# Expert products of layer 0: which scheduling turns may carry them

## The chip, the cores and the metric

The kernel runs on one core of a Trainium2 chip, as one launch. The metric is the device time of that launch in microseconds, from start to end, inputs and outputs in device memory. Three runs of the kernel before gave 3691.05, 3695.77 and 3702.05 us; their median, 3695.77 us, is the time to compare with.

## What is computed

The input is 16 samples of 512 tokens with 128 features in float32. Two layers follow each other. Cut to what matters:

```
xn = layernorm(x)
x  = x + memory(xn) + block0(xn)      # layer 0
xn = layernorm(x)
x  = x + attention1(xn) + moe1(xn)    # layer 1
```

- `memory` is a small two-layer network whose weights are updated over 8 chunks of 64 tokens, one after the other (a scan), and then read out.
- `block0` is a convolution over tokens, attention with 16 heads of width 8, a layernorm, and a dense mixture of 8 experts with 512 hidden units each: every token goes through every expert.
- `attention1` is causal attention with 16 heads, a convolution, and a second causal attention with the same keys and values.
- `moe1` sends each token to 8 of 32 small experts.

The dense mixture of layer 0 is what the change touches:

```
h = relu(einsum('bsd,edf->bsef', x, w1) + b1)
y = einsum('bsef,efd->bsed', h, w2) + b2
moe_out = einsum('bse,bsed->bsd', probs, y)
```

## The kernel before

The whole network is written as stages (Python generators), and a class `Turns` runs them. In every turn each live stage does one small step and gives control back. TensorE executes its instructions exactly in the order in which the turns issue them; so the list of turns, fixed when the program is built, is TensorE's program. There are 1279 turns. The launch falls into three parts: up to turn 520 the attention of layer 0 beside the scan; from turn 520 the attention of layer 1, with layer 0's expert products still going on; from turn 1140 the end of layer 1 and its own experts.

Within a turn the stages come in the order of a priority:

1. `tops` (priority 0) calls `largest`: two score matmuls of 64 rows (four or eight narrower ones near the causal corner), whose row maxima VectorE takes. In the profile these matmuls are `s<-kx,qx`. The maxima make the softmax safe.
2. `back` (priority 1) calls `weighted`: the same scores a second time, transposed, in the profile `s<-qx,kx`. ScalarE turns them into exponentials (line 470, tile `e`). The score tile has one buffer only (tag `p2`, `pools["p2"]` is 1), so the scores of the next turn cannot be written before ScalarE has read this turn's. In layer 1 GpSimd then cuts the causal corner (line 474).
3. Still in `weighted`, or in `summed` (priority 2) at the end of a head group, `tail` sums attention values: matmuls `pc<-e,vp`, one for each head, four or eight heads at once, when enough exponentials have gathered. A turn in which this happens puts the word `"values"` into `locks`. I call it a values turn, and any other turn a plain turn.
4. Other stages (priorities 3 to 5): the scan, projections, convolutions, layernorms, transposes.
5. `experts0` (priority 6) calls `ffn` for one sample after the other: the expert products.

One sample's expert products are 64 pieces: `first(i)` is a product of 128 hidden units for all 512 tokens (`phe<-x1T,ew`), followed by a relu on ScalarE (line 584) into `hTe`; `second(i)` multiplies that back to 128 features (`pye<-ew,hTe`, line 594), and every fourth one scales the sum by the gate on ScalarE (line 601) and adds it up on GpSimd (line 602). For 16 samples that is 1024 pieces. The two stand alternately: a `first`, then the `second` of the `first` before.

How many pieces a turn gets is decided in `ffn` by a credit. Each turn adds 2750 ns (`TURN`) to the credit and takes off `load_ns`, an estimate of the TensorE time of everything else in the turn; each piece takes off 1000, and the credit is capped at 4000, so at most four pieces are due at once. The kernel before then has two more rules. With `pools["pairs"]`, which is true throughout, the number of pieces is rounded down to an even one in plain turns, and set to zero in values turns unless four are due. And where the maxima of a turn keep VectorE longer than TensorE (`look_ns` against `load_ns`), pieces are added to fill the difference.

A last helper, `fill` (line 203), issues an otherwise useless matmul in turns with little TensorE work, but only when no expert stage has run for more than two turns.

Of the kernel before, what the change touches and what calls it, by code (L numbers as in the profile page):

```python
# [73 lines left out]
def bc(ap, axis, n):  # L74

    u = ap.unsqueeze(axis)
    shape = list(u.shape)
    shape[axis] = n
    return u.to_broadcast(shape)
# [3 lines left out]
def network(ctx: ExitStack, tc: tile.TileContext, a, out):  # L83
# [26 lines left out]
    def load(pool, name, shape):  # L110
        t = pool.tile(shape, F32, bufs=1, name="sb_" + name)
        nc.sync.dma_start(t, a[name])
        return t
# [22 lines left out]
    def col(name, i=0):  # L136
        k = COLS[name] + i
        return cols[:, k : k + 1]

    pools, done, locks, clock, newest, cleared, held, read, cell = {}, {}, set(), [0], [None], [None], [0], [0], []  # L140
# [3 lines left out]
    def mark(*m):  # L144
        done[m] = clock[0]

    def after(*marks, lag=0):

        while not all(m in done and clock[0] >= done[m] + lag for m in marks):
            yield  # L150
# [12 lines left out]
    def room():  # L163

        while held[0] >= pools["work"]:
            yield

    def hold(name):

        held[0] += 1  # L170
        return work(name)

    def drop():

        read[0] += 1

    def work(name):
        return pools["ps"].tile([P, 512], F32, tag="bank", bufs=5, name=name)

    def toks(ap):  # L180
        return ap.rearrange("p (t d) -> p t d", d=P)

    def flat(ap):
        return ap.rearrange("p t d -> p (t d)")

    load_ns, look_ns, array_ns, at_ffn = [0.0], [0.0], [0.0], [-9]

    def mm(o, lhsT, rhs, start=True, stop=True):
        n = int(np.prod(rhs.shape[1:]))
        if lhsT.dtype == FR:  # L190
            load_ns[0] += 0.5 * (0.45 * n + 105)
        else:
            t = 0.42 * n if lhsT.shape[-1] == 32 and n >= P else 2 * max(0.834 * n, 110)
            load_ns[0] += t
            array_ns[0] += t
        nc.tensor.matmul(o, lhsT=lhsT, rhs=rhs, start=start, stop=stop)  # L196
# [72 lines left out]
    def idle(n):  # L269
        for _ in range(n):  # L270
            yield
# [240 lines left out]
    credit, fetched = [0.0], {}  # L512
# [9 lines left out]
    def fetch0(b):  # L522

        x1T = ff.tile([P, S], F32, tag="x1T", bufs=1, name="x1T")
        nc.sync.dma_start(x1T, x1d[1, b])
        fetched[b] = x1T, {}, {}
        fetch1(*fetched[b][1:], 0)
        fetch2(*fetched[b][1:], 0)

    def ffn(b):  # L530

        yield from after(("x1", b))
        ac = ff.tile([P, TB, D], F32, tag="x1", bufs=1, name="ac")
        nc.sync.dma_start(flat(ac), x1d[0, b])
        if b not in fetched:
            fetch0(b)
            yield from idle(3)
        x1T, w1, w2 = fetched.pop(b)
        padded = gates0[b % 2]
        pr = padded[:, 0 : TB * EXP0].rearrange("p (t e) -> p t e", e=EXP0)  # L540
        prT = ff.tile([P, P], F32, tag="y", bufs=2, name="prT")

        def gate():
            yield from room()
            pgt = hold("pgt")[:, 0 : TB * EXP0].rearrange("p (t e) -> p t e", e=EXP0)
            for t in range(TB):
                mm(pgt[:, t, :], x1T[:, t * P : (t + 1) * P], gw0)
            yield
            mx = sm.tile([P, TB], F32, tag="mx", name="mx")
            nc.vector.tensor_tensor(pr, pgt, bc(row["gb"][:, 0:EXP0], 1, TB), ALU.add)  # L550
            drop()
            nc.vector.tensor_reduce(mx, pr, AX.X, ALU.max)
            nc.vector.tensor_tensor(pr, pr, bc(mx, 2, EXP0), ALU.subtract)
            yield
            nc.scalar.activation(pr, pr, AF.Exp)
            yield
            sp = sm.tile([P, TB], F32, tag="sp", name="sp")
            nc.vector.tensor_reduce(sp, pr, AX.X, ALU.add)
            nc.vector.reciprocal(sp, sp)
            nc.vector.tensor_tensor(pr, pr, bc(sp, 2, EXP0), ALU.mult)  # L560
            yield
            yield from room()
            ptp = work("ptp")
            nc.tensor.transpose(ptp[:, 0:P], padded, ident)
            nc.scalar.copy(prT, ptp[:, 0:P])
            yield from idle(2)
            yield from room()
            pb2 = work("pb2")
            mm(pb2, prT, eb2)
            y = ff.tile([P, TB, D], F32, tag="y", bufs=2, name="y")  # L570
            nc.scalar.copy(flat(y), pb2)
            nc.gpsimd.tensor_tensor(ac, ac, y, ALU.add)
            yield

        hs, pye, n = {}, [None], 4 * EXP0

        def first(i):
            e, f = divmod(i, 4)
            if e + 1 < EXP0 and f < 2:
                (fetch1, fetch2)[f](w1, w2, e + 1)  # L580
            ph = work("phe")
            mm(ph, w1[e][:, f * P : (f + 1) * P], x1T)
            hs[i] = ff.tile([P, S], F32, tag="hTe", bufs=3, name="hTe")
            nc.scalar.activation(hs[i], ph, AF.Relu, bias=col("fb", i))  # L584
            if i == n - 1 and ("x1", b + 1) in done:
                fetch0(b + 1)

        def second(i):
            e, f = divmod(i, 4)
            h = hs.pop(i)  # L590
            if f == 0:
                pye[0] = toks(hold("pye"))
            for t in range(TB):
                nc.tensor.matmul(  # L594
                    pye[0][:, t, :], lhsT=h[:, t * P : (t + 1) * P], rhs=w2[e][:, f, :],
                    start=(f == 0 and t == 0), stop=(f == 3), skip_group_check=True,
                )
            if f == 3:
                y = ff.tile([P, TB, D], F32, tag="y", bufs=2, name="y")
                for t in range(TB):  # L600
                    nc.scalar.mul(y[:, t, :], pye[0][:, t, :], pr[:, t, e : e + 1])  # L601
                nc.gpsimd.tensor_tensor(ac, ac, y, ALU.add)  # L602
                drop()

        units = [(first, 0)]
        for i in range(1, n):
            units += [(first, i), (second, i - 1)]
        units.append((second, n - 1))
        gating, at = gate(), 0
        while at < len(units):  # L610

            at_ffn[0] = clock[0]
            credit[0] = min(credit[0] + TURN - load_ns[0], 4000)
            more = int(max(credit[0] + 500, 0) // 1000)
            if pools["pairs"]:
                more = more // 2 * 2 if "values" not in locks or more > 3 else 0
            if credit[0] > -2000:

                more = max(more, int((look_ns[0] - load_ns[0] - 400) / 1000 + 0.7))
            for fn, u in units[at : at + more]:  # L620

                if held[0] >= pools["work"] - (fn is second and u % 4 == 0):
                    break
                fn(u)
                at += 1
                credit[0] -= 1000
            next(gating, None)
            yield
        yield
        nc.sync.dma_start(x1d[0, b], flat(ac))  # L630
        mark("ffn", b)
        yield
# [6 lines left out]
    att = main.enter_context(tc.tile_pool(name="att", bufs=1))  # L639
    fa = main.enter_context(tc.tile_pool(name="fa", bufs=2))  # L640
    ff = main.enter_context(tc.tile_pool(name="ff", bufs=1))
    ps = main.enter_context(tc.tile_pool(name="psum", bufs=1, space=PSUM))
    pools.update(ps=ps, p2=1, work=3, weights=[att], heads=4, pairs=True)
    Wt = Pack(load(fa, "pb", [P, sum(PB.values())]), PB)
    cell.append(Wt.t)
    row.update(load_rows(fa, "rows0", ROWS0))
# [485 lines left out]
    def experts0():  # L1132
        for b in range(B):
            yield from ffn(b)
# [26 lines left out]
        pass  # L1161
    for _ in padded_values(l1, 2):
        pass
    pools["pairs"] = True

    def middle(mid, b):

# [435 lines left out]
```

## Time and profile before

| What | Value |
|---|---|
| median of three runs | 3695.77 us |
| profiled execution, its own time | 3697.03 us |
| span in its profile | 3695.3 us |
| granted TensorE clock, mean | 0.970 |
| TensorE busy | 3466.2 us (94%) |
| VectorE / ScalarE / GpSimd busy | 62% / 58% / 43% |
| instructions | 62879 |

The span runs from the first to the last instruction; the profiled execution took 1.7 us more than its span. Busy shares are means over the three parts. "PE" is TensorE's matmuls, "PEld" its weight loads, "DVE" VectorE, "ACT" ScalarE, "POOL" GpSimd, "SP" the queue that issues most DMAs.

### The profile page before, as it was taken

To read this page: it belongs to the slowest core of one execution; us is meant where nothing else is said; L and a number is where in the kernel's file an instruction comes from. 1 tells how busy PE (TensorE), PEld (TensorE's weight loads), DVE (VectorE), ACT (ScalarE), POOL (GpSimd) and SP (SyncE) were. 2 spreads that over 40 slices of the span, in tenths; PEclk is the share of its full clock that TensorE was granted. 3 is DMA by queue.
4 is the path that set the end of the run, shared out by engine and by line. 5 is a ranking of instruction groups with operands and counts; after the bars stand their busy time and mean duration, and the time that the engine had idled before them with its cause. 6 is when DMAs were issued, how large, how long until landed. Compare 5 with 4: busy or idle time off the path is not lost. (4 is left out here: it accounts for less than half of the span.)

```text
span 3695.3 us, 62879 instructions
## 1 busy us (share of the span) xinstructions
PE 3466.2 (94%) x22209; PEld 1925.9 (52%) x22209; DVE 2283.0 (62%) x5907; ACT 2154.0 (58%) x3703; POOL 1571.3 (43%) x2524
## 2 busy tenths in 40 slices
PE   6999999899999899999999999999999999998877
PEld 3445554454555455455555555555555665443443
DVE  5676656556756565566466666666666666777652
ACT  1556756665656687666566666666666665443433
POOL 5433532442431455432444344434443444443664
PEclk7999999899999999999999999999999999998998
DMA  5222222222223233443434443444344334333343
GB/s 171 68 69 74 80 77 65 68 74 82 65 66 94 85 114 93 122 120 105 135 96 132 121 125 110 120 124 127 101 124 130 114 107 116 96 99 95 84 85 85
DMA packets 290074, 370.83 MB, mean 100 GB/s; under 512 B 46016, under 2 KB 141408, under 8 KB 289376
## 3 DMA queue, kind: packets, MB, share of 16 engines
q1 hardware_dynamic: 282592, 359.99, 34.0%
q0 software_dynamic: 7168, 6.82, 1.1%
q8 instruction: 177, 2.90, 0.3%
q14 instruction: 137, 1.12, 0.1%
HBM read 236.85 MB, written 133.25 MB: 100 GB/s over the span
## 5 line engine op out<-in xcount | busy, mean ns | idle before, releaser
L470 ACT ACTIVATE e<-s 128x1024 f32<-128x1024 f32 (+1 forms) x1216 | 1190.9, 979 | 667.7 <-PE s L196 587.0
L399 DVE TENSOR_REDUCE nm<-s 128x1 f32<-128x512 f32 (+2 forms) x1408 | 906.9, 683 | 527.0 <-PE s L196 525.6
L391 DVE CUSTOM_DVE_ANT_0 s<-s,sb_const 128x512 f32<-128x512 f32 (+1 forms) x1024 | 624.3, 643 | 444.3 <-PE s L196 436.3
L474 POOL TENSOR_SCALAR_AFFINE_SELECT e<-e 128x128 f32<-128x128 f32 (+2 forms) x1408 | 467.0, 367 | 865.9 <-ACT e L470 859.5
L196 PE MATMUL s<-kx,qx 64*128 64x512 f32 (+3 forms) x3072 | 657.3, 430 | 58.8 <-DVE nm L399 14.6
L196 PE MATMUL pc<-e,vp 128*32 128x512 f32 (+3 forms) x6144 | 657.2, 506 | 43.9 <-POOL e L474 41.8
L196 PEld LDWEIGHTS s<-kx,qx 64*128 64x128 f32 x3072 | 293.1, 187 | 627.9 <-issue 251.9
L594 PEld LDWEIGHTS pye<-ew,hTe 128*128 128x128 f32 x4096 | 517.7, 192 | 174.0 <-issue 159.5
L196 PE MATMUL s<-qx,kx 64*128 64x512 f32 (+3 forms) x3072 | 533.2, 360 | 39.4 <-ACT e L470 27.6
L594 PE MATMUL pye<-ew,hTe 128*128 128x128 f32 x4096 | 564.6, 281 | 0.8 <-ACT hTe L584 0.8
L196 PE MATMUL phe<-x1T,ew 128*128 128x512 f32 x1024 | 539.9, 612 | 8.4 <-DVE nm L399 6.4
L584 ACT ACTIVATE hTe<-phe,sb_cols 128x512 f32<-128x512 f32 x512 | 352.8, 690 | 280.5 <-PE phe L196 278.3
L602 POOL TENSOR_TENSOR ac<-ac,y 128x512 f32<-128x512 f32 x128 | 164.5, 1285 | 408.8 <-ACT y L601 380.9
L196 PEld LDWEIGHTS s<-qx,kx 64*128 64x128 f32 x3072 | 294.6, 189 | 82.0 <-ACT e L470 57.0
L398 DVE TENSOR_TENSOR s<-s,sb_const 128x256 f32<-128x256 f32 (+1 forms) x384 | 180.9, 516 | 230.6 <-PE s L196 224.9
L196 PEld LDWEIGHTS pc<-e,vp 128*32 128x32 f32 x6144 | 155.5, 110 | 285.5 <-issue 173.1
L196 PEld LDWEIGHTS phe<-x1T,ew 128*128 128x128 f32 x1024 | 157.7, 192 | 59.8 <-issue 34.2
L601 ACT ACTIVATE y<-pye,pr 128x128 f32<-128x128 f32 x512 | 146.8, 368 | 30.8 <-PE pye L594 25.8
L203 PE MATMUL fill<-sb_pb,sb_const 128*128 128x512 f32 (+2 forms) x324 | 148.4, 547 | 10.9 <-DMA sb_pb<-in_pb 10.3
L391 DVE DVE_READ_ACCUMULATOR2_ANT nm<- 128x1 f32 x1024 | 144.6, 141 | 0.0
L209 POOL TENSOR_SCALAR rs_t<-ss 128x4 f32<-128x4 f32 (+1 forms) x56 | 11.9, 213 | 238.8 <-ACT sq L262 235.1
L209 POOL TENSOR_SCALAR rs_t<-ln_mv 128x4 f32<-128x4 f32 x64 | 12.7, 198 | 178.7 <-DVE ln_mv L219 176.4
(292 smaller groups left out, 3856.0 us busy)
## 6 DMA issues: line engine op xcount, KB each, us to landing
ew<-in_ew SPq DMA_DIRECT2D x256, 256.0 KB
kx<-rk SPq DMA_DIRECT2D x192, 256.0 KB
qx<-rq SPq DMA_DIRECT2D x128, 256.0 KB
rq<-hi SPq DMA_DIRECT2D x64, 256.0 KB
rq<-lo SPq DMA_DIRECT2D x64, 256.0 KB
rk<-hi SPq DMA_DIRECT2D x64, 256.0 KB
rk<-lo SPq DMA_DIRECT2D x64, 256.0 KB
qx<-r SPq DMA_DIRECT2D x64, 256.0 KB
```

The source lines that it names most:

```text
L196: nc.tensor.matmul(o, lhsT=lhsT, rhs=rhs, start=start, stop=stop)
L203: nc.tensor.matmul(o[:, 0:n], lhsT=ident, rhs=cell[0][:, 0:n], start=True, stop=True)
L209: nc.gpsimd.tensor_scalar(t, src, scale, eps, ALU.mult, ALU.add)
L391: newest[0] = nc.vector.tensor_tensor_reduce(out=sv[r][:, 0, :], in0=sv[r][:, 0, :], in1=row["caus"][:, S - n :], scale=1.0, scalar=-BIG, ...
L398: nc.vector.tensor_tensor(dg, dg, bc(row["caus"][:, S - P :], 1, per), ALU.add)
L399: newest[0] = nc.vector.tensor_reduce(nm[:, qt, r, t : t + per], sv[r], AX.X, ALU.max)
L470: nc.scalar.activation(e[:, :, 0 : per * n], s[:, :, 0 : per * n], AF.Exp, scale=SCALE)
L474: cleared[0] = nc.gpsimd.affine_select(out=ev[:, r, :, 0:P], in_=ev[:, r, :, 0:P], pattern=[[0, per], [1, P]], compare_op=ALU.is_ge, fill= ...
L584: nc.scalar.activation(hs[i], ph, AF.Relu, bias=col("fb", i))
L594: nc.tensor.matmul(pye[0][:, t, :], lhsT=h[:, t * P : (t + 1) * P], rhs=w2[e][:, f, :], start=(f == 0 and t == 0), stop=(f == 3), skip_gro ...
L601: nc.scalar.mul(y[:, t, :], pye[0][:, t, :], pr[:, t, e : e + 1])
L602: nc.gpsimd.tensor_tensor(ac, ac, y, ALU.add)
```

## The change

Both extra rules go away and one takes their place. In a values turn, as many pieces as the credit says are due are issued, up to four and without rounding; since `ffn` has the lowest priority, they stand behind the value matmuls of that turn. In a plain turn pieces are issued only when four are due, and then four. The addition by `look_ns` is gone.

```diff
             credit[0] = min(credit[0] + TURN - load_ns[0], 4000)
             more = int(max(credit[0] + 500, 0) // 1000)
-            if pools["pairs"]:
-                more = more // 2 * 2 if "values" not in locks or more > 3 else 0
-            if credit[0] > -2000:
-
-                more = max(more, int((look_ns[0] - load_ns[0] - 400) / 1000 + 0.7))
+            if "values" not in locks and more < 4:
+                more = 0
             for fn, u in units[at : at + more]:
...
-    pools.update(ps=ps, p2=1, work=3, weights=[att], heads=4, pairs=True)
+    pools.update(ps=ps, p2=1, work=3, weights=[att], heads=4)
...
-    pools["pairs"] = True
```

## The prediction, made before the changed kernel ran

> **What bounds the kernel now.** I read the page's busy rows first, then the busy times of each part, then TensorE's timeline turn by turn. The page says that TensorE is nearly always busy, from shortly after the start to about 3100 us, and much less afterwards:
>
> ```profile
> PE 3466.2 (94%) x22209; PEld 1925.9 (52%) x22209; DVE 2283.0 (62%) x5907; ACT 2154.0 (58%) x3703; POOL 1571.3 (43%) x2524
> ...
> PE   6999999899999899999999999999999999998877
> ...
> PEclk7999999899999999999999999999999999998998
> ```
>
> The same by part. The first row runs from turn 520 to the last pieces, the second is the stretch right after them:
>
> ```profile
> 1604.00:3104.00 1500.00, 1474.51 (x10555) 876.57 (x10554) 923.81 (x2837) 926.12 (x1483) 616.26 (x1293) 1.00 0.42 119
> 3104.00:3290.00 186.00, 170.92 (x1187) 83.33 (x1185) 137.42 (x426) 91.52 (x117) 80.48 (x197) 0.94 0.38 102
> ```
>
> TensorE is busy 98% with pieces, 92% without, and there most plain turns carry a `fill`. So the pieces do not just add work: they stand where TensorE would otherwise wait. TensorE's timeline shows what for. Columns: start, duration, then instruction and count; a bracket is idle time and what ended it.
>
> ```profile
> 1774.79 0.51 PE L196 MATMUL s<-qx,kx 64*128 64x512 f32 x2
> 1775.23 0.66 PE L248 MATMUL tpc<-sb_const,cs 128*128 128x128 f32 x4
> 1776.49 0.51 PE L196 MATMUL s<-qx,kx 64*128 64x512 f32 x2 [0.61 <-ACT e L470]
> 1776.93 1.16 PE L594 MATMUL pye<-ew,hTe 128*128 128x128 f32 x8
> 1777.92 1.02 PE L196 MATMUL phe<-x1T,ew 128*128 128x512 f32 x2
> 1778.78 1.05 PE L594 MATMUL pye<-ew,hTe 128*128 128x128 f32 x8
> 1779.67 1.02 PE L196 MATMUL phe<-x1T,ew 128*128 128x512 f32 x2
> 1780.63 0.45 PE L196 MATMUL s<-qx,kx 64*128 64x384 f32 x2
> ```
>
> The second score pair waits 0.61 us because the exponential of the first still reads the only score buffer: 1.70 us from one pair to the next, however little TensorE has to do. After it four pieces fit before the next scores, from 1776.93 to 1780.63, with nothing waiting. Call the distance from scores to scores the exp cycle. Its parts are the pair (0.40), the exponential (1.02 for 1024 columns, 0.81 for the 384-wide turns) and two handovers (about 0.15 together). That is 1.6 us in layer 0 and about 1.5 in layer 1, where 4 of 11 turns are 384 wide; I use 1.55.
>
> ```profile
> 2202.95 0.49 PE L196 MATMUL s<-kx,qx 64*128 64x512 f32 x2
> 2203.28 0.34 PE L196 MATMUL s<-qx,kx 64*128 64x384 f32 x2
> 2203.55 1.16 PE L594 MATMUL pye<-ew,hTe 128*128 128x128 f32 x8
> 2204.54 1.02 PE L196 MATMUL phe<-x1T,ew 128*128 128x512 f32 x2
> 2205.49 0.50 PE L196 MATMUL s<-kx,qx 64*128 64x512 f32 x2
> ```
>
> This is the commonest plain turn before: both score pairs and a pair of pieces, 2205.49 - 2202.95 = 2.54 us (2.55 is the median of such turns). The exponential runs under the pieces and costs nothing. The same turn with four pieces lasts 4.31 us (2085.3 to 2089.6, for one), so a further piece costs (4.31 - 2.55)/2 = 0.88 us. The bare scores take 0.60 (2202.95 to 2203.55), which leaves 2.55 - 0.60 - 1.76 = 0.19 us for going into a group of pieces and out of it.
>
> **The change part by part.** The turns are the same 1279 in the same order; only pieces move. The instruction order of the two programs, cut into turns, gives:
>
> - pieces in values turns: 57 before, 741 after; in plain turns 967 before, 283 after (sum 1024 both)
> - values turns that carry pieces: 46 and 277; plain turns that do: 426 and 75
> - last piece: turn 1057 and turn 1080, still ahead of turn 1140, where the last sample's next stage starts; that delay costs nothing
> - plain turns with no piece: 237 more than before, up to turn 1080. Of them, 186 have nothing but scores on TensorE (59 before turn 520, 127 after), 91 have a little more (mostly the 256- and 128-wide score turns), 70 have at least 1.5 us of other work (some emptied turns are offset by others filled, so these are net counts by kind).
>
> *A bare turn emptied of a pair.* It falls from 2.55 to the exp cycle, 1.55: minus 1.00. Its two pieces go behind values, where TensorE has no slack (a values turn with eight heads spends 1.92 us on `pc` beside the scores), and cost 2 x 0.88 = 1.76. Net +0.76 us, the group overhead of 0.19 saved in it. The gap is counted once per emptied turn, so a turn that lost four counts the same. 186 x 0.76 = 141 us.
>
> *A turn with a little more.* The 256-wide pair turns lasted 2.98, so their own work is about 1.0; emptied they fall to 1.55: -1.43 + 1.76 = +0.33. The 128-wide ones lasted 2.82. In the stretch without pieces eight of them took a median of 2.06 (VectorE ends those): -0.76 + 1.76 = +1.0, at least +0.5 if 1.55 holds. The rest of this kind gain or lose nothing. With roughly 27, 33 and 31 turns of the three sorts: 9 + 33 + 0, about 41 us.
>
> *The 70 others.* Their own TensorE work exceeds the cycle; a pair cost 1.7 there, as behind values. Zero.
>
> *What else moves with the pieces.* Relu and gate scaling go with them on ScalarE: 0.69 for each `first`, four times 0.29 for each expert sum. They lie ahead of the next exponential in ScalarE's queue. Before, pieces hid that; now a relu that trails its values turn ends before the next scores do (0.9 us of scores), but a trailing gate scaling delays the exponential by about 0.3, in at most 128 places: 0 to 38 us, I take 15. GpSimd's cut of the causal corner gets less cover before the values that need it. The stretch without pieces shows it, `pc` waiting 0.85 us:
>
> ```profile
> 3106.55 0.99 PE L196 MATMUL pc<-e,vp 128*32 128x256 f32 x8 [0.85 <-POOL e L474]
> ```
>
> It cost 2.7 us in 30 values turns there; over 190 in layer 1, 17 us, between 0 and 60. The 256 expert weight loads move on SP with their pieces. Each is asked for at least seven pieces ahead, now about two values turns or 17 us; no wait on them shows in the trace, and I cost them at nothing. If that cover went, each landing would be paid on TensorE. Twelve `fill`s fewer: nothing.
>
> **A rule against the row: the clock.** The trace shows the clock halved after a thin window, although the gap in it was short:
>
> ```profile
> 3173.90:3177.30 3.40, 1.14 (x18) 0.38 (x10) 1.65 (x6) 0.94 (x1) 1.22 (x2) 1.00 0.56 119
> 3177.30:3180.70 3.40, 3.34 (x6) 1.34 (x8) 0.00 (x0) 1.02 (x1) 0.54 (x2) 0.50 1.08 239
> 3180.70:3184.10 3.40, 3.40 (x26) 1.90 (x28) 1.95 (x4) 1.61 (x2) 0.54 (x2) 0.50 0.30 51
> ```
>
> TensorE had been busy 1.14 of 3.40 us, with one gap of 2.32. The Trainium skill ("TensorE: Matmul & The Clock Gate", section "HAM oscillation — how this bites in real kernels") asks only that no idle gap pass about 3.4 us. By the rule the new gaps, about 1 us each, cost nothing. By the row a thin window is enough. A lone emptied turn between two values turns leaves the window about two thirds full; two in a row, 23 times in layer 1, may leave it thin. Half of these at 3.4 us of half clock: 12 x 1.7 = 20 us. If all 226 gaps counted half the time it would be 190. I go with the row and take 10.
>
> A second page speaks for the change ("TensorEngine Tiling (Array Packing)", "Key Properties"): changing the tiling mode drains TensorE. Scores (64*128), values (128*32) and pieces (128*128) are three modes; by my count about 450 changes fewer. The row prices a group's entry and exit at 0.19 us, and that is already in the +0.76. By the rule alone, with TensorE never waiting, the sum would be a gain (third rival).
>
> Sum: 141 + 41 + 15 + 17 + 10 = 224, less about 25 for emptied turns whose gap falls into a wait that exists already (PE waits for 15 us on ACT e and 11 on DVE nm in the first part): +200 us. From the profiled execution's 3697 that is 3897; the median lies 1 us lower, so 3896.
>
> **The rivals.**
>
> 1. *The exp cycle is only half exposed* (9%): other work follows the scores more often than I counted, and the first part hides its 59 gaps behind the scan. Then about +90, 3786. For it: the first part has waits of up to 10 us. Against: layer 1 has almost none, and holds two thirds of the sum.
> 2. *The clock joins in* (15%): thin windows halve it after most emptied turns, +60 to +190 on top: 3950 to 4080. For it: the rows above. Against: scores keep TensorE more than half busy in the cycle.
> 3. *Fewer mode changes win* (4%, faster): 351 plain groups dissolve at 0.19 us, 231 groups join values at perhaps half of that: -67 + 22 = -45, 3651. It decides if TensorE can use the emptied time, which needs an exp cycle under about 0.8 us instead of 1.55. The wait of 0.61 above says no.
> 4. *No change to measure* (2%): the cycle's cost and the saved mode changes cancel.
>
> **How the numbers follow.** The main case has 70%, with its own range from 3800 to 3990. Taking in the first rival and the lower part of the second, 3790 to 4010 leaves out about 2 in 10. About 0.3% is what a measurement here can tell from no change. Slower 0.94, within it 0.02, faster 0.04.
>
> **What would show it.** TensorE busy falls from 98% to about 90% in the part from turn 520 on, with new entries "PE s <- ACT e" of some 100 us in the waits, where 10.7 stood; plain bare turns at 1.5 to 1.7 us, values turns at 4 to 6. ScalarE and VectorE keep their busy times. It is wrong if that wait stays small, if the clock in that part falls well under 1.00, or if the loss lies before turn 520.

## The result: 3963 us, 7.1% slower

| Kernel | Median | Lowest to highest | Runs |
|---|---|---|---|
| before | 3698.91 us | 3691.05 to 3703.94 | 4 |
| changed | 3962.86 us | 3961.11 to 3969.10 | 4 |

The ratio is 1.0711 (95% interval 1.0699 to 1.0724): 264 us lost where +200 was forecast, inside the range of 3790 to 4010.

The three parts, cut at the first score matmul of turns 90, 520 and 1058 in each trace:

| Part | Before | Changed | Difference |
|---|---|---|---|
| turns 90 to 520 | 1347.0 us | 1395.0 us | +48.0 |
| turns 520 to 1058 | 1499.7 us | 1692.6 us | +192.9 |
| turn 1058 to the end | 591.0 us | 614.6 us | +23.6 |

Pieces moved between the parts too. The first part has 308 pieces before and 307 after, the second 716 and 685, the end none and 32. So the middle loses its 193 us with 31 pieces less to do (about 27 us at 0.88 each), and the +23.6 at the end comes with 32 more (about 28).

### The profile page after: what moved, and what is told of

It is laid out like the page before. It is cut to its first block, busy times and chain, and to the rows that moved or that the text cites. A ratio compares the mean times of both kernels' runs of the same rounds, so it can differ in the third digit from the quotient of the medians.

```text
span 3959.7 us, 62838 instructions
## 1 busy us (share of the span) xinstructions
PE 3550.3 (90%) x22185; PEld 1973.2 (50%) x22185; DVE 2265.3 (57%) x5907; ACT 2160.7 (55%) x3703; POOL 1578.9 (40%) x2524
## 5 line engine op out<-in xcount | busy, mean ns | idle before, releaser
L196 PE MATMUL s<-kx,qx 64*128 64x512 f32 (+3 forms) x3072 | 684.7, 423 | 93.2 <-issue 32.7
L196 PE MATMUL pc<-e,vp 128*32 128x512 f32 (+3 forms) x6144 | 685.5, 526 | 40.6 <-POOL e L474 40.4
L196 PE MATMUL s<-qx,kx 64*128 64x512 f32 (+3 forms) x3072 | 559.6, 376 | 179.2 <-ACT e L470 165.6
L594 PEld LDWEIGHTS pye<-ew,hTe 128*128 128x128 f32 x4096 | 529.2, 194 | 235.2 <-issue 208.9
L196 PEld LDWEIGHTS s<-kx,qx 64*128 64x128 f32 x3072 | 318.4, 188 | 563.6 <-issue 272.3
L203 PE MATMUL fill<-sb_pb,sb_const 128*128 128x512 f32 (+2 forms) x300 | 140.1, 558 | 10.9 <-DMA zrow<-zero 10.4
```

What stands on the lines that cost most here:

```text
L203: nc.tensor.matmul(o[:, 0:n], lhsT=ident, rhs=cell[0][:, 0:n], start=True, stop=True)
L594: nc.tensor.matmul(pye[0][:, t, :], lhsT=h[:, t * P : (t + 1) * P], rhs=w2[e][:, f, :], start=(f == 0 and t == 0), stop=(f == 3), skip_gro ...
```

## The profile after

The page's busy rows, with the 40 slices of TensorE. TensorE has slightly more busy time than before and a lower share, and the steady level 9 of the middle is gone:

```profile
PE 3550.3 (90%) x22185; PEld 1973.2 (50%) x22185; DVE 2265.3 (57%) x5907; ACT 2160.7 (55%) x3703; POOL 1578.9 (40%) x2524
...
PE   6999999989999999988989889889898889998887
```

The same stretch as before, from turn 520 to 1058, is now:

```profile
1652.00:3345.00 1693.00, 1511.47 (x10392) 887.52 (x10391) 902.97 (x2834) 915.43 (x1452) 617.03 (x1292) 0.97 0.37 105
```

TensorE was idle for 1500.0 - 1474.5 = 25.5 us there before and is idle for 1693.0 - 1511.5 = 181.5 now. So 156 of the 193 us are waiting. Busy time rose by 37 although 31 pieces left, so the work that stayed takes some 64 us longer; the clock column, 0.97 instead of 1.00, belongs here. VectorE, ScalarE and GpSimd do nearly what they did.

What TensorE waited for in that stretch (total us, times, longest):

```profile
PE s L196 <- ACT e L470: 105.6, 158, 1.4
PE s L196 <- issue: 31.1, 20, 1.6
PE s L196 <- DVE nm L399: 12.4, 21, 1.6
PE s L196 <- DVE nm L391: 6.0, 12, 0.6
...
PE pc L196 <- POOL e L474: 2.1, 2, 1.2
```

Before, the first of these lines was:

```profile
PE s L196 <- ACT e L470: 10.7, 13, 1.2
```

The exponential holds scores up for 105.6 us instead of 10.7. A second group, 31.1 + 12.4 + 6.0 = 49.5 us, is first scores that wait for a bank which VectorE's maxima have not yet given back. The view puts the 31.1 us under "issue", to no engine; but each of these 20 waits, 1.51 to 1.58 us long, ends 0.10 us after a maximum of VectorE (line 399) has ended. So of the 156 us of new waiting about 95 end with the exponential and nearly 50 with VectorE.

From one values turn to the next on TensorE's timeline (the bracket is idle time and its end):

```profile
2092.11 0.44 PE L196 MATMUL s<-kx,qx 64*128 64x384 f32 x2
2092.39 0.40 PE L196 MATMUL s<-qx,kx 64*128 64x256 f32 x4
2092.63 0.33 PE L196 MATMUL s<-kx,qx 64*128 64x384 f32 x2
2093.99 0.66 PE L196 MATMUL s<-qx,kx 64*128 64x128 f32 x8 [1.03 <-ACT e L470]
2094.58 1.07 PE L196 MATMUL pc<-e,vp 128*32 128x256 f32 x16
2095.59 1.12 PE L196 MATMUL phe<-x1T,ew 128*128 128x512 f32 x2
2096.55 1.05 PE L594 MATMUL pye<-ew,hTe 128*128 128x128 f32 x8
2097.44 1.02 PE L196 MATMUL phe<-x1T,ew 128*128 128x512 f32 x2
```

A plain turn issues its two score groups (2092.11 and 2092.39), the next turn's maxima scores follow at once (2092.63), and then nothing can be done for 1.03 us: from 2092.39 to 2093.99, one exp cycle of 1.60 us. Then come values and three pieces, all without a gap. At the same place in the kernel before, four pieces stood between the two score groups, and the values turn behind them carried none:

```profile
1999.07 0.40 PE L196 MATMUL s<-qx,kx 64*128 64x256 f32 x4
1999.40 1.12 PE L196 MATMUL phe<-x1T,ew 128*128 128x512 f32 x2
2000.36 1.05 PE L594 MATMUL pye<-ew,hTe 128*128 128x128 f32 x8
2001.25 1.02 PE L196 MATMUL phe<-x1T,ew 128*128 128x512 f32 x2
2002.11 1.05 PE L594 MATMUL pye<-ew,hTe 128*128 128x128 f32 x8
...
2003.37 0.56 PE L196 MATMUL s<-qx,kx 64*128 64x128 f32 x8
```

Without them the turn shrank from 4.30 to 1.60 us, which is 2.70 less; four pieces at 0.88 elsewhere cost 3.52.

## The experiments

**The rule in one part only.** The kernel before with the new rule from turn 520 on.

```diff
+            if clock[0] >= 520:
+                if "values" not in locks and more < 4:
+                    more = 0
+            else:
                 ...
```

> The new rule from turn 520 on, the old one before it. If the loss is made turn by turn, by emptied plain turns, the parts add: turns 90 to 520 last 1347 us as before, turns 520 to 1058 about 1690 as in the changed kernel, the end as in the changed kernel; in all 3699 + 193 + 23 = 3915 us. Rival: the parts depend on each other (the pieces that the first part leaves over set what the second suffers); then the second part differs from 1690 by more than 20 us.

3906.80 us (ratio 1.0582, interval 1.0551 to 1.0613). The parts lasted 1347.4, 1694.5 and 608.0 us: the first as in the kernel before, the second as in the changed kernel. That is 213 us over the runs of the kernel before beside it, where 216 was forecast: the loss adds up part by part.

**One half of the change: values turns take what is due, plain turns keep their pairs.**

```diff
-                more = more // 2 * 2 if "values" not in locks or more > 3 else 0
+                more = more // 2 * 2 if "values" not in locks else more
```

> The kernel before with one part of the change alone: values turns take whatever is due, plain turns keep pairs and the VectorE addition. 335 pieces behind values, 7 bare and 18 slightly fuller plain turns emptied. Theory: 7 x 0.76 + 18 x 0.45 = +13 us, 3710. Rival (price per piece behind values): 41% of the loss, +107 us.

3718.75 us (1.0069, 1.0048 to 1.0090): +25 us, twice the forecast of the theory and a quarter of the rival's. With 335 pieces behind values instead of 57, nearly all of the loss is absent: standing there is not by itself what costs.

**The other rule relaxed: plain turns from two due pieces on.**

```diff
-            if "values" not in locks and more < 4:
+            if "values" not in locks and more < 2:
                 more = 0
```

> The changed kernel, but plain turns take pieces when two are due, not only when four are. Pieces behind values fall from 741 only to 322 (57 in the kernel before), but plain turns without pieces fall nearly to the number before: net 20 bare and 42 slightly fuller ones more than before. Theory (the price is paid per emptied plain turn): 20 x 0.76 + 42 x 0.45 = +34 us over the kernel before, up to +50 with the clock: about 3735. Rival (the price is paid per piece that stands behind values, through long turns): 39% of the loss, +102 us, 3800.

3728.84 us (1.0097, 1.0079 to 1.0114): +35 us. With nearly half as many pieces behind values as the changed kernel has, seven eighths of the loss are gone. The wait for the exponential in turns 520 to 1058 is 13.2 us.

**The VectorE addition alone taken out of the kernel before.**

```diff
-            if credit[0] > -2000:
-
-                more = max(more, int((look_ns[0] - load_ns[0] - 400) / 1000 + 0.7))
```

> The kernel before without the addition of pieces under VectorE's maxima; pairs and values turns as before. 12 bare and 2 fuller plain turns emptied. Theory: +10 us, 3705. Rival (VectorE paces the turns, and the addition is what hid that): +50 us or more.

3711.24 us (1.0044, 1.0029 to 1.0058): +17 us. The addition is worth a little, more than the theory said, far from the rival's 50. By parts the trace shows 15.5 us less in turns 90 to 520, 31.7 more in turns 520 to 1058 and 7.7 less at the end, so it seems to help in the middle alone; with one trace this is not more than a hint.

**The exponential made longer, in both kernels.**

```diff
             nc.scalar.activation(e[:, :, 0 : per * n], s[:, :, 0 : per * n], AF.Exp, scale=SCALE)
+            nc.scalar.activation(e[:, :, 0:P], s[:, :, 0:P], AF.Exp, scale=SCALE)
```

> The changed kernel with a second exponential over 128 columns of each half (the same values once more, about 0.38 us) before the score buffer is free. Theory: the exp cycle paces every plain turn without pieces, so about 310 light turns in which the cycle binds get 0.38 us longer each: +118 us over the changed kernel, 4081. Rival: the loss comes from the clock or from more and larger groups behind values; then it costs no more than in the kernel before (0 to 30 us).

> The kernel before with the same second exponential. Theory: a plain turn with a pair lasts 2.55 us, longer than the lengthened cycle of about 1.95, so only turns that are bound already pay: +10 to +40 us, 3710 to 3740. Rival: ScalarE's work counts in itself, and both kernels lose alike.

4194.15 us (1.1349, 1.1320 to 1.1378) and 3811.06 us (1.0313, 1.0291 to 1.0336): the same exponential more in each turn, 0.385 us, cost the changed kernel 231 us and the kernel before 118. In turns 520 to 1058 it was 1829.3 - 1692.6 = 137 against 1544.0 - 1499.7 = 44, three to one. First the waits of that stretch in the changed kernel with the longer exponential, then those of the kernel before with it:

```profile
PE s L196 <- ACT e L471: 191.0, 196, 1.9
```

```profile
PE s L196 <- ACT e L471: 30.5, 55, 1.6
```

The cycle paces the changed kernel much more than the one before, as the theory says. It shows most plainly turn by turn in that stretch. From one exponential's scores to the next, 169 bare turns without a piece grew from 1.61 to 1.97 us in the changed kernel, nearly the whole 0.385. In the kernel before, 166 bare turns with a pair went from 2.63 to 2.65.

Both amounts are about 100 us above the forecast. In the changed kernel part of the 137 us is the clock: with the longer exponential TensorE spent 228.7 us of the stretch at half clock, against 99.0. In the kernel before, the start and the three parts lost 7, 44, 44 and 20 us in the profiled execution. In turns 90 to 520, 48 values turns with four heads and no other work grew by 0.38 us each, so they are paced by the cycle too, and I had thought of plain turns only.

**Fills in the emptied turns.** The changed kernel with a small fill matmul in light plain turns without a piece, meant to fit into the wait and keep TensorE busy. (`placed` is set where a piece is issued and cleared at the end of a turn.)

```diff
-        if clock[0] - at_ffn[0] > 2 and n > 0 and held[0] < pools["work"]:
+        if clock[0] - at_ffn[0] <= 2:
+            n = min(n, 256) if "values" not in locks and not placed[0] else 0
+        if n > 0 and held[0] < pools["work"]:
```

> The changed kernel with a fill matmul of up to 256 columns (about 0.55 us) in each plain turn that has no piece and less than 0.86 us of float32 work; it fits into the wait for the exponential. Theory: the loss is 156 us of waiting and some 40 us of halved clock in turns 520 to 1058; then the clock there goes from 0.97 back to 0.99 or more and the time falls by about 40 us, to 3920, while the wait for the exponential stays. Rival: the waits are all of it and the thin windows came at moments when TensorE waited anyway; then the time stays at 3963 or rises a little.

> The changed kernel with fills of up to 384 columns (about 0.84 us) instead of 256 in the light plain turns. With 256 columns the halved time in turns 520 to 1058 fell from 99 to 48 us and that part from 1693 to 1672 us, 0.41 us for each us of halved time. If the clock costs that much throughout, the halved time falls under 20 us and the part to about 1660, 3920 in all. Rival: scores and fill together (1.45 us) begin to fill the exp cycle themselves; then the clock is whole but the part is no shorter than 1672.

3932.57 us (1.0650, 1.0625 to 1.0675) and 3928.53 us (1.0621, 1.0601 to 1.0640). The part from turn 520 to 1058, kernel by kernel:

| Fill | Time at half clock | Length |
|---|---|---|
| none (changed kernel) | 99.0 us | 1692.6 us |
| 256 columns | 47.8 us | 1671.6 us |
| 384 columns | 23.9 us | 1668.1 us |

With 256 columns, TensorE's busy time and clock in that part:

```profile
1651.00:3323.00 1672.00, 1614.40 (x10837) 945.00 (x10836) 911.44 (x2838) 915.21 (x1453) 614.64 (x1292) 0.99 0.37 106
```

TensorE is busy 97% again, and the kernel is hardly faster. 75 us less of halved clock brought 24.5 us, 0.33 for each; at that rate the clock has about 33 of the 193 us. That is too little, because the fills cost something themselves. The 384 columns fell short of the forecast of 1660: emptied bare turns went from 1.48 us on average to 1.53 with 256 columns and 1.60 with 384, the rival in part. Over 209 turns with a fill, compared one by one with the changed kernel, that added 5.5 and 15.2 us, while turns that had met a halved stretch in either trace lost 29.2 and 36.7, about half a microsecond for each at half clock. By this the clock has about 50 of the 193 us. The remaining 140 stay while TensorE is busy: a busy row can be filled with work of no use.

**The score buffer in two halves.** To shorten the exp cycle itself, in both kernels, with the same memory:

```diff
-            s = pools["ps"].tile([P, 2, 512], F32, tag="p2", bufs=pools["p2"], name="s2")
+            s = [pools["ps"].tile([P, 512], F32, tag="p2", bufs=2, name="s2") for r in range(2)]
...
-            nc.scalar.activation(e[:, :, 0 : per * n], s[:, :, 0 : per * n], AF.Exp, scale=SCALE)
+            for r in range(2):
+                nc.scalar.activation(e[:, r, 0 : per * n], s[r][:, 0 : per * n], AF.Exp, scale=SCALE)
```

> The changed kernel with the score buffer of the exponentials cut into its two banks, each a tile of its own with its own exponential of 512 columns (about 0.60 us each, worked out from 0.385 for 256 and 1.025 for 1024). The next scores of the first half can be written while ScalarE still reads the second, so the exp cycle falls from 1.6 to about 1.25 us although ScalarE has 0.18 us more to do per turn. Theory (the waiting is for the one score buffer): some 310 light plain turns gain up to 0.3 us, 3963 falls by 60 to 95 us, to about 3885. Rival (VectorE's maxima, or long values turns in themselves): no gain, or a loss of up to 50 us by the extra work.

> The same cut in the kernel before. Pieces already stand in the cycle there; only bound turns gain (about 50 values turns with four heads in the first part, and 25 us of waits in the second), and ScalarE does 219 us more that lies beside TensorE: 3675 to 3700. Rival: ScalarE's extra work delays relus and copies that TensorE waits for: 3710 to 3750.

3971.68 us (1.0715, 1.0686 to 1.0744) and 3715.37 us (1.0028, 1.0015 to 1.0041): no gain in the changed kernel, the rival's number (the forecast was 60 to 95 us less), and none in the kernel before. The waits of turns 520 to 1058 moved, though; these are the changed kernel's with halves:

```profile
PE s L196 <- ACT e L471: 48.1, 116, 1.1
PE s L196 <- DVE nm L399: 27.8, 29, 1.6
PE s L196 <- issue: 14.0, 9, 1.6
```

From scores to scores, a bare emptied turn fell from a mean of about 1.5 to 1.1 us, and a values turn with three pieces rose from 4.9 to 5.2 (turns at full clock). The reason is inside the pair. The first half starts earlier, but the second must wait for the second exponential, and that ends later than the one exponential did (2 x 0.575 us on average against 0.98). Over the whole run, in 160 of 381 values turns with a plain score pair the second score came over 0.3 us after the first, against 39 in the changed kernel. The profile counts such a gap inside a pair as busy: in turns 520 to 1058 TensorE's idle time fell by 55 us and its busy time rose by 60, of which 46 are these gaps. Values need both halves, so ahead of a values turn the way through the last half is what counts, and the cut does not shorten it. So this run did not take the wait away, and its forecast was wrong on that; it tells nothing against the theory or for it. A second whole score buffer, which would take the wait away, was not tried.

The same trace names VectorE for one of the waits that the changed kernel's view had left as "issue", at the 128-wide score turns:

```profile
2461.79 0.46 PE L196 MATMUL s<-kx,qx 64*128 64x512 f32 x1 [1.58 <-DVE nm L399]
```

**A version that might beat both: less credit per turn.** In the kernel before, `TURN` at 2700 and 2650 instead of 2750.

> The kernel before with the credit per turn at 2700 instead of 2750 ns: the pieces end at turn 1090 instead of 1057, and some that stood in turns with other work now stand in turns that had a fill. Theory: an emptied turn costs nothing where its own work exceeds the cycle, and a piece in a bare turn at the end costs under half of its time: -5 to -20 us, 3680 to 3692. Rival (an even spread was already the best): 0 to +10.

> The kernel before with a credit of 2650 ns per turn; the last piece moves to turn 1133, seven turns ahead of where it would delay the last sample. Theory: the part up to turn 1058 shortens further and the end lengthens by nearly as much; with 2700 the sum was -6 us, here -5 to -15: 3680 to 3690. Rival: the pieces at the end now stand in turns where they cost their full time; then it is 3694 or more.

3687.72 us (0.9978, 0.9967 to 0.9989, 12 runs) and 3702.57 us (1.0009, 0.9997 to 1.0022, 12 runs). With 2700 the parts lasted 1328.4, 1496.8 and 602.4 us; the pieces at the end cost less than they free. It is 0.2% faster than the kernel before: the interval leaves out 1, but the gain is under the 0.3% that the prediction named as what can be told. With 2650 the end, from that program's own turn 1058, grows to 626.6 us and the gain is gone. There more than pieces moved: from 434 us on the scores themselves come in another order.

## Why the prediction was right, step by step

*What bounds.* The exp cycle was read off one wait of 0.61 us, and it is what emptied turns fall to. By the distance from one exponential's scores to the next, the same turns in both traces at full clock, bare turns of turns 520 to 1058 went from 2.57 (with a pair) to 1.48 us on average, against 1.55 assumed. Longer exponentials lengthen just these turns, and kernels with few emptied turns lose little, with up to 335 pieces behind values.

*The prices by kind.* 256-wide turns fell from 3.17 to 1.95 us, and 128-wide ones from 2.85 to 2.09: -1.22 and -0.76 where -1.43 and -0.76 were taken. "The 70 others: zero" held as well: 56 emptied turns with 0.8 us or more of other TensorE work fell by a median of 1.75 us, just what a pair was taken to cost behind values. Values turns with three pieces last about 4.9 us. As forecast, the wait for the exponential is near 100 us in that part, TensorE's share there is 89%, and VectorE and ScalarE nearly keep their busy times. Of the three signs of being wrong one came in part: the clock of that part fell to 0.97.

*The terms that were mis-sized.*

- The clock: 10 us taken, about 50 found, by the fills. The direction taken from the row was right and its size too small: 26 halvings where I had 12 thin windows in mind, counting only double gaps. Half of the halvings, 13, follow on one of the 20 long waits for VectorE, which the sum did not have.
- "The group overhead of 0.19 saved": it is mostly paid again behind values. At full clock, 88 values turns that went from no piece to three grew by 2.79 us, 0.15 more than 3 x 0.88. Over all values turns that gained, a piece cost 0.906 instead of 0.88; for 684 pieces that is 18 us.
- "Less about 25" for gaps that fall into existing waits of the first part: there the wait for the exponential rose from 14.7 to 55.1 us, and the part lost 48 us; 59 x 0.76 = 45 were to be expected without any discount. The discount was wrong.
- GpSimd's cut ahead of the values: 17 us taken, 2.1 us of wait found in turns 520 to 1058.

These four make 40 + 18 + 25 - 15 = 68, where 264 - 200 = 64 us were missing. That they meet so well is partly luck: bare turns fell by up to 0.1 us more than taken, and the 15 us for trailing gate scalings could not be read off either trace. One count in the working does not fit the rest. It names 237 turns newly without a piece, but its counts by kind add up to 347, and the turns with pieces fell by 426 - 75 = 351. The sum was built on the counts by kind, so it does not change.

*The rivals.* The clock does join in, but as about a quarter of the middle's loss. The first part did not hide its gaps. Fewer changes of tiling mode brought no net gain in time. VectorE, priced only inside the 128-wide turns, holds scores up for 49.5 us: it ends a third of the new waiting. The trace shows this wait, but no run took it away by itself in the changed kernel, so its share of the time stays open, and so does that of the exponential against it.

## What to carry to other kernels

When a chain with one buffer sets a floor under each turn, work that does not depend on it belongs inside the floor, a little in every turn; behind the turns that are full already it is paid in full, and the floor is paid as well. Before moving work, ask what its old place was hiding: a busy engine's work may be free where it is. And count by place, not by sum: the pieces' total was the same here, and the number of turns left without one told the loss.

## What was not expected of the hardware

The clock was halved 26 times in turns 520 to 1058 of the changed kernel, although the longest gap ahead of any of them was 2.71 us. In the 3.41 us ahead of each halving TensorE was busy for a median of 1.80 us, and the longest gap had a median of 1.52. What tells the windows apart is their busy share. The changes of the clock lie on a grid of 3.41 us; of the windows at full clock on this grid, 20 of the 23 that were busy less than 60% were followed by a halving, and 6 of the 443 that were busier. Here is one, in stretches of 3.4 us; the middle one runs at half clock, and the sixteen value matmuls that begin in it take 3.60 us where 1.92 was the rule:

```profile
2452.10:2455.50 3.40, 1.69 (x17) 1.06 (x21) 3.19 (x6) 1.02 (x1) 1.09 (x4) 1.00 0.86 222
2455.50:2458.90 3.40, 3.40 (x17) 0.55 (x16) 1.87 (x8) 0.81 (x1) 0.60 (x2) 0.50 0.53 102
2458.90:2462.30 3.40, 3.40 (x25) 2.59 (x23) 0.00 (x0) 0.90 (x2) 0.00 (x0) 1.00 0.25 67
```

The Trainium skill ("TensorE: Matmul & The Clock Gate", "HAM oscillation — how this bites in real kernels") warns of gaps over about 3.4 us; in this trace a window about half busy was mostly enough, with no gap of that length. Each us at half clock cost about half a us by the fills, so 99 us of it are about a quarter of the loss of that part.
